# Bias and relu of a feed-forward moved to ScalarE, the 8-bit copy to VectorE, and a new table of times

## The chip, the cores and the metric

The kernel runs on one core of one Trainium2 chip. A core has five engines that run on their own: TensorE (PE in the profile, with its weight loads as PEld), VectorE (DVE), ScalarE (ACT), GpSimd (POOL) and SyncE (SP), which here issues nearly all DMAs. Each engine is given its instructions in the order in which the program records them; between engines, semaphores make a reader wait for its writer and a writer for the last reader of what it overwrites. The metric is the device time of the program in microseconds, the median of several runs.

## The reference

The input is 64 images of 96 channels, 56 x 56. Layer 0 is a convolution block: a 1x1 expansion to 192 channels with silu, a shift and shuffle of channel groups, a depthwise 3x3, silu, a squeeze-and-excite gate, a 1x1 projection and a residual. Layer 1 takes the 3136 pixels as tokens, normalizes them, mixes them in a two-dimensional frequency domain (here as matrix products with tables), and adds that to the tokens. The last part is a quantized feed-forward:

```python
def _qlinear(x, W, b):
    y = q_acc(jnp.einsum('bsk,nk->bsn', q_mul(x), q_mul(W)))   # 8 bit in, sum rounded to 16 bit
    return q_acc(y + q_mul(b))                                 # sum with the bias, rounded to 16 bit
h = jax.nn.relu(_qlinear(x, W1, b1))                           # 96 -> 384
y = _qlinear(h, W2, b2)                                        # 384 -> 96
```

`q_mul` rounds to a float with 5 exponent and 2 mantissa bits (fp8e5), `q_acc` to one with 5 and 10 (f16). So the hidden layer needs, in this order: the product rounded to f16, the bias added and rounded to f16, relu, and a rounding to fp8e5 for the second product.

## The kernel before

The work on an image is cut into some 60 kinds of steps, each a small function with an image number `b` and a part number `i`. Names end in `_mm` for matrix products on PE, and mostly in `_ev` for the evictions of their results from PSUM. The stages, in the order of an image's way through them:

- `x_in`, `ea_mm`, `ea_ev`, `eb_mm`, `eb_ev`, `eb_sh`, `eb_z`: load, expansion with silu (ACT); `eb_sh` shifts channel groups by DMAs on SP, `eb_z` clears border columns on POOL.
- `dw_mm`, `dw_ev`, `gt`, `gs`, `lt`, `ls`: the depthwise filter, in part as PE products, in part as nine taps each on DVE (`gt` L489 and L487, `lt` L502 and L500); the sums in `dw_ev`, `gs`, `ls` go to the gate.
- `se1_*`, `se2_*`: the gate. `se2_pw` (L552, DVE) folds it into the projection's weights, once per image.
- `pj_mm`, `pj_add` (L587, DVE), `pj_ev` (L593, ACT): projection and residual, into the token tile `t`.
- `c_mm`, `c_st`, `c_v`, `c_pow`, `sp_v` (L655, DVE), `sp_mm`, `sp_ev`, `sp_st`: statistics of the first normalization, in two halves; `c_pow` is a power on POOL.
- `w1_mm`, `w1_ev` (L686, DVE), `f1_mm`, `f1_ev`, `f1_st`: first mix, first transform, results to DRAM.
- `f2_ld` (SP), `f2_mm`, `f2_u` (L770, ACT), `f2_s` (L786 and L789, DVE), `f2_r` (L793, ACT), `f2_p` (L799, DVE): second transform with a complex product and relu, in six groups. A group has a tile `ue` with two halves, which `f2_u` writes one after the other and `f2_s` reads and rewrites.
- `w2_*`, `i1_*`, `i2_ld` (SP), `i2_mm`, `i2_ev` (L896, DVE): second mix and the way back, added to `t`.
- `n_*`, `x_*`: second normalization, tokens as fp8e5 (`n_pow` L912 on POOL, `n_x` L919 on ACT).
- the feed-forward, in 7 groups of 8 rows with 3 parts each, so 21 times per image: `h_mm` (L939, PE), `h_ev` (L944, ACT: PSUM to 16 bit), `h_b` (L949), `h_q` (L955); then per group `o_mm` (L961, PE), `o_ev` (L966, ACT), `o_b` (L971, ACT: second bias, in 16 bit), `o_f` (L977, DVE: residual), `o_st` (SP).

Before, `h_b` adds the bias and takes the maximum with 0 on DVE, in place on the 16-bit tile, and `h_q` copies that tile to fp8e5 on ACT.

The order of all steps is written in a table. `PLAN` has for every step and part a time, and `PERIOD` the distance of two images; all steps of all 64 images are recorded in the order of `b * PERIOD + when`:

```python
for _, b, k, i in sorted(
    (b * PERIOD + when, b, k, i)
    for b in range(NB)
    for k, step in enumerate(STEPS)
    for i, when in enumerate(PLAN[step.__name__])
):
    STEPS[k](b, i)
```

So the times are only sort keys: nothing waits for a clock. With times from -9 to 428 and a PERIOD of 105, parts of five images are interleaved on each engine, and one pass through the order, from one `se2_pw` to the next, holds each step of an image once. The PSUM tiles are few: two large buffers are used in turn by `w1`, `f1`, `f2`, `w2`, `i1` and `i2`, and four small ones in turn by all other products.

Of the kernel before, what the change touches and what calls it, by code (L numbers as in the profile page):

```python
# [10 lines left out]
AF = mybir.ActivationFunctionType  # L11
ALU = mybir.AluOpType
# [29 lines left out]

PERIOD = 105.0000000
PLAN = {
    "x_in": (-5.6038637, -8.8381554, 6.2538794, 1.1812168, 16.3290193, 18.2852724, 6.8664140),
    "ea_mm": (71.3166402, 9.9626057, 70.7451177, 21.6750117, 65.3314579, 73.1081582, 53.0001125),
    "ea_ev": (71.4998900, 11.8833092, 70.9831361, 25.0494290, 65.3324579, 75.4760214, 54.7839542),
    "eb_mm": (20.7568939, 18.2862724, 20.0880579, 17.7349364),  # L50
    "eb_ev": (23.7980033, 19.7804381, 20.6194508, 17.7359364),
    "eb_sh": (30.1373485, 40.4268576, 27.1837130, 37.9131670),
    "eb_z": (47.6742308,),
    "dw_mm": (77.9546249, 77.9556249, 80.7234624),
    "dw_ev": (84.6664508, 84.5735370, 85.4255761, 84.6664508),
    "gt": (
        72.3773055, 76.5125929, 80.2867409, 80.6441083, 81.5978867, 83.3027644, 84.6020247, 85.5619425, 86.6358385,
    ),
    "gs": (87.3111062,),
    "lt": (  # L60
        47.4152368, 51.7884497, 60.4614124, 63.7966655, 70.3566676, 70.7623183, 72.0563386, 78.2533320, 82.6592559,
    ),
    "ls": (84.0968675,),
    "se1_mm": (88.1632442,),
    "se1_ev": (88.3332823,),
    "se2_mm": (89.5466763,),
    "se2_ev": (90.4665288,),
    "se2_th": (90.7934716,),
    "se2_pw": (92.0502895,),
    "pj_mm": (94.5530355, 94.5540355, 102.0867331, 102.0877331),  # L70
    "pj_add": (95.2755331, 97.5636980, 96.0830143, 95.1836140, 106.8994545, 105.9451741, 104.6876054, 105.6968155),
    "pj_ev": (95.9050131, 100.2006242, 96.8964656, 97.4087014, 107.1621768, 108.5177420, 105.3642695, 105.8415338),
    "c_mm": (108.8639612, 112.5088807, 112.0440542, 109.4090967, 116.6350776, 116.2904132, 135.7736125),
    "c_st": (109.9566474, 113.8485179, 113.0437550, 111.6043666, 127.2877074, 117.1026522, 137.4879453),
    "c_v": (113.8495179, 141.3061112),
    "c_pow": (113.8505179, 141.3071112),
    "sp_v": (118.0429167, 144.9541062),
    "sp_mm": (119.0531042, 154.1921897),
    "sp_ev": (120.1871679, 157.1439845),
    "sp_st": (130.9824656, 157.1449845),  # L80
    "w1_mm": (140.5452441, 132.6482511, 135.8336192, 137.4906636, 166.3523765, 171.4972169, 172.4722919),
    "w1_ev": (143.0235958, 134.1359263, 138.9251145, 141.6196817, 167.5676600, 175.3749595, 176.4038215),
    "f1_mm": (145.6274382, 150.9380879, 155.6433445, 167.0161422, 169.8440182, 175.7343775, 181.4398534),
    "f1_ev": (147.8032262, 153.3968496, 159.4311586, 168.6496602, 170.8773139, 175.7353775, 183.1217269),
    "f1_st": (156.9268876, 156.9278876, 159.7610134, 170.1776408, 177.2523722, 181.0963765, 183.4782115),
    "f2_ld": (187.2815556, 187.2825556, 187.2835556, 188.6871659),
    "f2_mm": (191.1567314, 194.9032982, 192.7760178, 198.9093529, 201.4926219, 207.3412304),
    "f2_u": (
        191.1577314, 191.6562889, 197.1245553, 197.1783541, 193.2014504, 193.4636961, 199.3778915, 199.4257855,
        202.6220676, 205.9228992, 210.6728919, 211.5690444,  # L90
    ),
    "f2_s": (
        192.4250284, 193.9349638, 197.4091017, 197.4101017, 194.5789035, 195.6210358, 199.5749065, 199.8323547,
        205.9228992, 207.2409149, 211.9521364, 211.9531364,
    ),
    "f2_r": (193.9359638, 199.3441286, 197.3984294, 206.6372292, 207.5062232, 214.4127396),
    "f2_p": (196.9933570, 199.5074020, 198.4889191, 207.7927174, 209.1210238, 217.7061307),
    "w2_mm": (200.3894916, 200.0698788, 211.3168798, 219.8206887),
    "w2_ev": (201.9237699, 200.2428780, 213.5686424, 221.6127349),
    "i1_mm": (203.1484168, 217.0192486, 223.8701013),  # L100
    "i1_ev": (207.4757051, 209.2393192, 221.2926416, 218.5724351, 226.9503254, 225.7919736),
    "i1_st": (227.4371665, 231.7746699, 237.1127120),
    "i2_ld": (247.3246163, 258.4005613),
    "i2_mm": (247.3256163, 248.9786662, 258.4015613, 258.4015613),
    "i2_ev": (248.8862636, 249.1565727, 251.6982706, 252.2464870, 259.1359643, 258.4025613, 264.6426220, 261.8850697),
    "n_mm": (253.7316943, 255.9231087, 254.3994689, 265.3165318, 262.8490081, 267.4335438, 274.2854929),
    "n_sq": (253.7326943, 256.4684950, 254.9830489, 267.2212265, 263.8196833, 269.2996327, 274.6498815),
    "n_v": (253.7336943, 257.7773358, 255.3268787, 271.2717974, 268.7188670, 272.3139830, 278.4419729),
    "n_pow": (253.7346943, 262.7040095, 256.0602786, 275.1413670, 271.5489182, 273.1976811, 278.5569536),
    "n_x": (259.5582250, 262.7050095, 260.5027085, 276.7536912, 273.5135570, 275.1181728, 279.4588576),  # L110
    "x_mm": (259.5592250, 267.5155107, 260.5037085, 277.7892684, 276.4517499, 277.1023738, 280.0425162),
    "x_ev": (262.4788526, 271.3250083, 262.9497100, 279.9343023, 277.5776996, 279.5752541, 280.9231813),
    "h_mm": (
        282.1072054, 281.8171435, 284.3242143, 283.3068688, 297.0889770, 299.9198326, 301.6559190, 316.8088320,
        330.1509260, 345.7814283, 348.2910018, 350.2353211, 296.8878517, 323.5297033, 341.8803208, 341.1070144,
        349.1164583, 347.9208679, 316.7096209, 337.5767067, 324.7962443,
    ),
    "h_ev": (
        284.9055256, 281.8181435, 286.7711359, 286.2538800, 300.1659528, 301.6061574, 301.6569190, 319.9246149,
        331.0399476, 346.4058862, 354.2442780, 353.1416746, 297.2413855, 326.1086749, 343.4780845, 342.6875640,  # L120
        356.9377387, 352.1488917, 318.6795915, 341.2226048, 328.4873812,
    ),
    "h_b": (
        285.4467375, 285.0084677, 291.2143255, 290.3869640, 307.4021554, 308.1480888, 315.5861436, 337.9149029,
        341.4422638, 351.7638454, 354.2452780, 353.3258891, 302.2808169, 326.8831223, 346.3774903, 342.6885640,
        357.2985996, 352.4379170, 320.6635037, 341.2236048, 337.0905654,
    ),
    "h_q": (
        290.1888952, 290.1898952, 292.3650273, 291.6620769, 314.5146883, 319.2434525, 328.1869035, 340.6025047,
        344.9455204, 354.3021981, 356.7052110, 375.6421815, 326.8831223, 326.8841223, 346.3869475, 346.7213238,  # L130
        374.1067707, 366.6357739, 325.5334877, 345.8789179, 337.3330982,
    ),
    "o_mm": (297.2153719, 323.2068041, 391.0564841, 383.7794044, 346.7502251, 401.7878092, 346.4614096),
    "o_ev": (299.2426704, 325.5592410, 392.9287695, 385.0364968, 346.9425985, 404.8006504, 346.4624096),
    "o_b": (302.4327810, 325.5602410, 395.0955840, 397.1802374, 347.8135349, 407.2015543, 351.0696253),
    "o_f": (325.1830475, 327.1074074, 398.6818786, 400.3662261, 357.3959208, 411.4278754, 351.6615662),
    "o_st": (340.2945764, 339.2746723, 424.0034698, 405.1739043, 379.1046584, 427.6733014, 390.2778445),
}


# [1 line left out]
def conv_attn_ffn(  # L142
# [36 lines left out]
    nc = tc.nc  # L179
# [157 lines left out]
    qb1 = const.tile([128, 3], F32, name="qb1")  # L337
# [40 lines left out]
    held = {}  # L378
# [567 lines left out]

    def h_b(b, i):
        y16 = held["y", b, i]
        nc.vector.tensor_scalar(y16, y16, qb1[:, i % 3 : i % 3 + 1], 0.0, ALU.add, ALU.max)  # L949

    def h_q(b, i):
        j, m = divmod(i, 3)
        if m == 0:
            held["h8", b, j] = work.tile([128, 3, CH], F8, tag="h8", name="h8", bufs=3)
        nc.scalar.copy(held["h8", b, j][:, m, :], held.pop(("y", b, i)), saturate=False)  # L955

    def o_mm(b, j):
        h8 = held.pop(("h8", b, j))
# [21 lines left out]
    def o_st(b, j):  # L980
# [6 lines left out]
        w1_mm, w1_ev, f1_mm, f1_ev, f1_st, f2_ld, f2_mm, f2_u, f2_s, f2_r, f2_p, w2_mm, w2_ev, i1_mm, i1_ev, i1_st,  # L987
        i2_ld, i2_mm, i2_ev,
        n_mm, n_sq, n_v, n_pow, n_x, x_mm, x_ev, h_mm, h_ev, h_b, h_q, o_mm, o_ev, o_b, o_f, o_st,
    )  # L990

    with tc.manual_schedule():
# [3 lines that stand above are left out]
# [183 lines left out]
```

## Time and profile before

| | us |
|---|---|
| three runs | 6437.04, 6433.02, 6433.70 |
| median | 6433.7 |
| the profiled execution | 6434.72 |
| its span, first to last instruction | 6432.9 |
| PE busy | 5903.3 |
| DVE busy | 5452.4 |
| ACT busy | 5003.9 |
| POOL busy | 1159.1 |

The mean granted clock of TensorE was 0.984. Rows of the profile name a line of the kernel, an engine, an operation, the tile written and those read, the shape, a count, then busy time and the mean of one in ns, and the idle time of the engine in front of such instructions with what ended it. Rows of a timeline give the start in us from the span's beginning, the length in us, and then the instruction; "x2" merges two in a row.

### The profile page before, as it was taken

Reading aid. Unit: us, or ns where it says so; the run is one execution under the profiler, and the core shown is the slowest. Engines: PE = TensorE matmul, PEld = TensorE weight load, DVE = VectorE, ACT = ScalarE, POOL = GpSimd, SP = SyncE. Lnnn points to the kernel's source line nnn. Section 1 sums busy time; section 2 is a strip of 40 time slices with the busy share of each in tenths; the row PEclk is TensorE's granted clock in tenths of the full one; section 3 lists DMA queues with packets and bytes.
Section 4 is the critical chain, followed back from the end, with each engine's and each line's share of the span. In section 5 each row is a group of like instructions: output and inputs, shape, how many; then the busy total and the mean of one; then the engine's idle time right before and its main releaser. Section 6 shows DMA issues by size and latency. Waiting matters only on the chain.

```text
span 6432.9 us, 215622 instructions
## 1 busy us (share of the span) xinstructions
PE 5903.3 (92%) x92162; PEld 3939.1 (61%) x92162; DVE 5452.4 (85%) x10386; ACT 5003.9 (78%) x10830; POOL 1159.1 (18%) x652
## 2 busy tenths in 40 slices
PE   5999999999999999999999999999999999999996
PEld 3666666666666666666666666666666666666664
DVE  6788888888888888888988888888888888888885
ACT  2677778778777787777787787878877877878777
POOL 1112112112112111121121121211211211211211
PEclk8999999999999999999999999999999999999997
DMA  3344434444444444344444443443443444444433
GB/s 93 109 117 127 125 110 133 122 118 127 121 122 127 115 127 125 110 131 119 117 129 123 121 126 113 130 121 113 132 125 112 130 124 117 127 117 129 121 108 92
DMA packets 665511, 772.70 MB, mean 120 GB/s; under 512 B 273104, under 2 KB 591256, under 8 KB 664424
## 3 DMA queue, kind: packets, MB, share of 16 engines
q1 hardware_dynamic: 661832, 757.14, 41.8%
q8 instruction: 724, 11.86, 0.8%
q10 hardware_dynamic: 2720, 1.77, 0.1%
q14 instruction: 235, 1.93, 0.1%
HBM read 349.05 MB, written 354.16 MB: 109 GB/s over the span
## 4 chain that ended last, share of the span: by engine, by line
DVE 29%; PE 27%; ACT 13%; POOL 12%; DMA 11%; issue 5%; SPq 2%; POOLq 0%; DVEq 0%; ACTq 0%
POOL rs L912 8%; DVE d_vec L489 7%; DMA buf_g<-rows 6%; POOL rs L650 4%; PE psa L849 4%; DMA buf_g<-spec 4%; DVE t L896 3%; DVE d_last L502 3%; DVE ue L789 3%; DVE s L786 3%; ACT ue L770 3%; PE ps_pj L568 3%; PE psa L810 2%; PE ps_pj L579 2%; PE ps_eb L415 2%
## 5 line engine op out<-in xcount | busy, mean ns | idle before, releaser
L650 POOL TENSOR_TENSOR rs<-v,mhalf 128x16 f32<-128x16 f32 (+1 forms) x128 | 384.7, 3006 | 4385.6 <-DVE v L645 4385.6
L955 ACT CAST h<-y 128x448 fp8e5<-128x448 f16 x1344 | 749.0, 575 | 286.8 <-DVE y L949 286.8
L502 DVE SCALAR_TENSOR_TENSOR d_last<-e_b,taps,d_last 128x1568 f32<-128x1568 f32 x512 | 944.0, 1844 | 0.5
L912 POOL TENSOR_TENSOR rs<-v,mhalf 128x4 f32<-128x4 f32 x448 | 741.7, 1760 | 818.9 <-DVE v L617 784.0
L489 DVE SCALAR_TENSOR_TENSOR d_vec<-e_a,taps,d_vec 128x1120 f32<-128x1120 f32 x512 | 707.1, 1381 | 2.7
L949 DVE TENSOR_SCALAR y<-y,qb 128x448 f16<-128x448 f16 x1344 | 424.9, 329 | 324.8 <-ACT y L944 318.0
L944 ACT CAST y<-ps_h 128x448 f16<-128x448 f32 x1344 | 674.6, 539 | 26.9 <-PE ps_h L939 26.9
L681 PE MATMUL psa<-w1c,t 112*128 112x192 f32 x3584 | 669.0, 330 | 2.8 <-DMA t<-dev_t 2.8
L468 PE MATMUL ps_d<-e_a,diag 32*32 32x504 f32 x18432 | 628.6, 590 | 1.5 <-issue 1.4
L681 PEld LDWEIGHTS psa<-w1c,t 112*128 112x128 f32 x3584 | 592.5, 190 | 22.4 <-ACT fs L713 3.0
L468 PEld LDWEIGHTS ps_d<-e_a,diag 32*32 32x32 f32 x18432 | 410.5, 103 | 200.7 <-ACT y L944 37.3
L745 PE MATMUL psa<-l_tab,buf_g 128*64 128x112 f32 x7424 | 425.3, 267 | 113.9 <-DMA buf_g<-spec 87.9
L745 PEld LDWEIGHTS psa<-l_tab,buf_g 128*64 128x64 f32 x7424 | 369.5, 140 | 250.4 <-DMA buf_g<-spec 131.5
L919 ACT ACTIVATE xt<-ps_n,rs 128x96 fp8e5<-128x96 f32 x1792 | 454.4, 346 | 72.5 <-POOL rs L912 65.9
L686 DVE SCALAR_TENSOR_TENSOR buf_h<-psa,rs 128x768 f32<-128x768 f32 x448 | 425.5, 950 | 55.0 <-PE psa L681 54.6
L977 DVE TENSOR_TENSOR o<-t,o 112x448 f32<-112x448 f32 x448 | 418.8, 935 | 21.8 <-ACT o L971 19.5
L786 DVE SCALAR_TENSOR_TENSOR s<-psa,fa,ue 128x448 f32<-128x448 f32 (+1 forms) x512 | 325.2, 635 | 117.3 <-ACT ue L770 112.8
L593 ACT ACTIVATE t<-ps_pj,pjbn_b 112x504 f32<-112x504 f32 (+1 forms) x512 | 300.5, 619 | 150.2 <-DVE ps_pj L587 150.2
L400 PE MATMUL ps_ea<-x,ex_w 112*32 112x448 f32 x3584 | 416.1, 550 | 0.0
L770 ACT ACTIVATE ue<-psa,fa 128x448 f32<-128x448 f32 (+1 forms) x512 | 336.5, 686 | 100.0 <-DVE buf_h L799 57.7
L701 PE MATMUL psa<-buf_h,f_tab 56*64 56x384 f32 x3584 | 395.2, 509 | 17.6 <-DVE t L896 9.3
L810 PE MATMUL psa<-w2a,buf_h 128*64 128x96 f32 (+1 forms) x7424 | 358.9, 248 | 50.2 <-ACT buf_g L840 34.0
(171 smaller groups left out, 11865.9 us busy)
## 6 DMA issues: line engine op xcount, KB each, us to landing
spec<-fs SPq DMA_DIRECT2D x448, 384.0 KB
buf_g<-spec SPq DMA_DIRECT2D x192, 672.0 KB
out_dram<-o SPq DMA_DIRECT2D x448, 196.0 KB
buf_g<-rows SPq DMA_DIRECT2D x128, 672.0 KB
x<-in_x SPq DMA_DIRECT2D x320, 203.0 KB
rows<-buf_g SPq DMA_DIRECT2D x128, 420.0 KB
rows<-buf_g SPq DMA_DIRECT2D x64, 504.0 KB
x<-in_x SPq DMA_DIRECT2D x128, 228.4 KB
```

The lines of the kernel that those rows point to most:

```text
L468: nc.tensor.matmul(pss[r][j * 32 : j * 32 + 32], lhsT=diag[pr, tap, :], rhs=e_a[pr, r0 : r0 + SR, dx : dx + HW], start=tap == 0, stop=tap ...
L489: nc.vector.scalar_tensor_tensor(d_vec, win, w, d_vec, ALU.mult, ALU.add)
L502: nc.vector.scalar_tensor_tensor(d_last, win, w, d_last, ALU.mult, ALU.add)
L650: nc.gpsimd.tensor_tensor(rs[:, js], v[:, js], mhalf[:, js], ALU.pow)
L681: nc.tensor.matmul(ps[:, k, 0:MID], lhsT=t[:, n0 : n0 + 2 * TP], rhs=w1c, start=True, stop=True)
L745: nc.tensor.matmul(ps[c0 : c0 + 64, k, 0:CP], lhsT=g_v[:, k1, c0 : c0 + 64], rhs=l_tab[:, k1, :], start=True, stop=True,)
L770: nc.scalar.activation(held["ue", b, i][:, q, 0:n, :], held["f2", b, i][:, 0:n, 0:HW], AF.Identity, bias=par[:, 2 + q : 3 + q], scale=par[ ...
L786: nc.vector.scalar_tensor_tensor(held["s", b, i][:, q, 0:n, :], im, par[:, m : m + 1], a, ALU.mult, ALU.add)
L810: nc.tensor.matmul(ps[c0:c1, u, k, 0:C], lhsT=pq_a[:, AT[k1], c0:c1], rhs=w2a, start=k == 0, stop=False, skip_group_check=True,)
L912: nc.gpsimd.tensor_tensor(rs, held.pop(("nv", b, g)), mhalf[:, 0:4], ALU.pow)
L944: nc.scalar.copy(y16, held.pop(("h", b, i)))
L955: nc.scalar.copy(held["h8", b, j][:, m, :], held.pop(("y", b, i)), saturate=False)
```

## The change

`h_b` becomes an ACT activation, relu with the bias as its argument, in place on the same 16-bit tile; `h_q` becomes a DVE copy from that tile to fp8e5. The names and lines stay. `PERIOD` and the times of all steps in `PLAN` are new; `pj_mm` keeps its four parts. The diff, with the table cut to the rows of which the text speaks:

```diff
-PERIOD = 105.0000000
+PERIOD = 102.2951152
 PLAN = {
...
-    "eb_sh": (30.1373485, 40.4268576, 27.1837130, 37.9131670),
-    "eb_z": (47.6742308,),
+    "eb_sh": (-17.6154500, -15.9127200, -24.0315800, -15.6905400),
+    "eb_z": (-7.7850900,),
...
-    "c_mm": (108.8639612, 112.5088807, 112.0440542, 109.4090967, 116.6350776, 116.2904132, 135.7736125),
+    "c_mm": (59.4587800, 60.0115300, 62.0418600, 60.7653300, 67.0208600, 62.6719000, 65.2556000),
...
-    "sp_v": (118.0429167, 144.9541062),
+    "sp_v": (68.5601600, 79.5835800),
...
-    "w1_ev": (143.0235958, 134.1359263, 138.9251145, 141.6196817, 167.5676600, 175.3749595, 176.4038215),
+    "w1_ev": (80.9797500, 83.0191200, 93.3324800, 87.2346800, 105.1838200, 111.0812800, 97.2977000),
...
     "f2_u": (
-        191.1577314, 191.6562889, 197.1245553, 197.1783541, 193.2014504, 193.4636961, 199.3778915, 199.4257855,
-        202.6220676, 205.9228992, 210.6728919, 211.5690444,
+        138.0540500, 138.0550500, 147.6787200, 148.3315400, 140.6491200, 142.2848100, 150.8378500, 151.8766800,
+        154.9088200, 155.0511900, 159.5374300, 160.6034600,
     ),
     "f2_s": (
-        192.4250284, 193.9349638, 197.4091017, 197.4101017, 194.5789035, 195.6210358, 199.5749065, 199.8323547,
-        205.9228992, 207.2409149, 211.9521364, 211.9531364,
+        140.3886900, 140.3896900, 149.4147700, 150.2843900, 143.5489500, 143.7516700, 151.6466600, 152.4316700,
+        155.3184000, 156.4887900, 161.3532300, 161.3542300,
     ),
...
-    "i2_ld": (247.3246163, 258.4005613),
+    "i2_ld": (180.1612300, 188.5926300),
...
-    "i2_ev": (248.8862636, 249.1565727, 251.6982706, 252.2464870, 259.1359643, 258.4025613, 264.6426220, 261.8850697),
+    "i2_ev": (185.9837900, 185.9837900, 186.7002400, 187.1144600, 191.7293400, 191.1283000, 195.0233515, 194.8050300),
...
     "h_ev": (
-        284.9055256, 281.8181435, 286.7711359, 286.2538800, 300.1659528, 301.6061574, ...
+        229.1094900, 228.7612101, 239.7382600, 228.8131600, 244.2390900, 246.5362800, ...
     "h_b": (
-        285.4467375, 285.0084677, 291.2143255, 290.3869640, 307.4021554, 308.1480888, ...
+        230.6722300, 236.0710000, 242.1428400, 233.1143800, 249.6670900, 258.1373100, ...
...
-    "o_b": (302.4327810, 325.5602410, 395.0955840, 397.1802374, 347.8135349, 407.2015543, 351.0696253),
+    "o_b": (283.1918300, 273.6047100, 352.4743700, 303.5309500, 292.8660900, 336.4152500, 287.7771600),
-    "o_f": (325.1830475, 327.1074074, 398.6818786, 400.3662261, 357.3959208, 411.4278754, 351.6615662),
+    "o_f": (286.8041800, 279.1551200, 358.2985100, 313.3837400, 297.8003600, 339.2981000, 289.8053900),
...
@@ def h_b, def h_q
     def h_b(b, i):
         y16 = held["y", b, i]
-        nc.vector.tensor_scalar(y16, y16, qb1[:, i % 3 : i % 3 + 1], 0.0, ALU.add, ALU.max)
+        nc.scalar.activation(y16, y16, AF.Relu, bias=qb1[:, i % 3 : i % 3 + 1])
 
     def h_q(b, i):
         j, m = divmod(i, 3)
         if m == 0:
             held["h8", b, j] = work.tile([128, 3, CH], F8, tag="h8", name="h8", bufs=3)
-        nc.scalar.copy(held["h8", b, j][:, m, :], held.pop(("y", b, i)), saturate=False)
+        nc.vector.tensor_copy(held["h8", b, j][:, m, :], held.pop(("y", b, i)), saturate=False)
```

On DVE the order of one pass is, around the places of which the text speaks: before, `sp_v[0]` h_b 20, c_st 4, h_b 7, 19, 8, 15, w1_ev 1, h_b 14, c_st 6, w1_ev 2, c_v 1, w1_ev 3, o_f 6, h_b 9, 17, w1_ev 0, h_b 11, `i2_ev[0]`; after, `sp_v[0]` h_q 6, 7, 19, o_f 1, h_q 20, 13, c_v 1, sp_v 1, h_q 14, w1_ev 0, o_f 0, w1_ev 1, h_q 15, 17, 16, `i2_ev[0]`.

On SP, before: sp_st 0, i1_st 2, eb_sh 2, eb_sh 0, i2_ld 0, eb_sh 3, eb_sh 1, i2_ld 1; after: i1_st 2, sp_st 0, o_st 2, o_st 1, i2_ld 0, eb_sh 2, eb_sh 0, i2_ld 1, eb_sh 1, eb_sh 3. On POOL, before: n_pow 0, n_pow 2, eb_z, n_pow 1; after: n_pow 0, n_pow 2, n_pow 1, eb_z.

## The prediction

> **What bounds the kernel now.** I read the engine sums first, then the chain that ended last.
>
> ```profile
> span 6432.9 us, 215622 instructions
> PE 5903.3 (92%) x92162; PEld 3939.1 (61%) x92162; DVE 5452.4 (85%) x10386; ACT 5003.9 (78%) x10830; POOL 1159.1 (18%) x652
> DVE 29%; PE 27%; ACT 13%; POOL 12%; DMA 11%; issue 5%; SPq 2%; POOLq 0%; DVEq 0%; ACTq 0%
> ```
>
> No engine is full, and the chain passes through all of them: a fixed order on each engine is waiting round a loop. The loop is one image. The instruction at L552 (`se2_pw`) runs once per image, 64 times, from 82.0 to 6241.7 us, so an image takes 6159.7 / 63 = 97.8 us, and 82.0 before and 191.2 after lie outside the loop. I cut one undisturbed image, from L552 to L552, at two joints where the chain changes engines: `sp_v` (L655, first half) and the first `i2_ev` (L896).
>
> ```profile
> 4087.03:4119.66 32.63, 30.47 (x405) 19.54 (x401) 27.42 (x70) 25.07 (x45) 3.77 (x1) 1.00 0.35 105
> 4119.66:4134.50 14.84, 14.17 (x149) 10.09 (x150) 8.83 (x28) 12.40 (x27) 2.27 (x1) 1.00 0.71 167
> 4134.50:4184.37 49.87, 47.37 (x890) 31.21 (x887) 48.48 (x64) 40.79 (x97) 11.84 (x8) 0.97 0.43 123
> ```
>
> Columns after the length: PE, weight loads, DVE, ACT, POOL busy. Stretch A (32.6) is a ping-pong of PE, DVE and ACT. In B (14.8) DVE is 60% busy and ACT 84%. In C (49.9) DVE is busy 48.5: **C lasts as long as its DVE work**, and has 1.4 of idle. So DVE work moved from B to C is not free, though DVE as a whole has 12.6 us of idle per image (97.34 - 84.73).
>
> The waits that matter, from the timelines of ACT and DVE in this image (start, length, what, idle before):
>
> ```profile
> 4087.14 1.34 ACT L770 ACTIVATE ue<-psa,fb 128x448 f32<-128x448 f32 x2 [0.79 <-DVE buf_h L799]
> 4092.40 1.34 ACT L770 ACTIVATE ue<-psa,fa 128x448 f32<-128x448 f32 x2 [0.90 <-DVE buf_h L799]
> ```
> ```profile
> 4088.52 0.69 DVE L786 SCALAR_TENSOR_TENSOR s<-psa,fb,ue 128x448 f32<-128x448 f32 x1 [0.39 <-ACT ue L770]
> 4093.77 0.68 DVE L786 SCALAR_TENSOR_TENSOR s<-psa,fa,ue 128x448 f32<-128x448 f32 x1 [0.40 <-ACT ue L770]
> 4125.84 0.83 DVE L949 TENSOR_SCALAR y<-y,qb 128x448 f16<-128x448 f16 x3 [4.85 <-ACT y L944]
> ```
>
> The first `f2_s` of a group starts not behind the first `f2_u`, but behind **both**: the two end at 4087.14 + 1.34 = 4088.48, and DVE starts at 4088.52; again 4093.74 and 4093.77. Both halves share one tile `ue`, and an access waits for all earlier writes of the tile. The third line is the big hole of B.
>
> **The moved operations, priced.**
>
> ```profile
> L955 ACT CAST h<-y 128x448 fp8e5<-128x448 f16 x1344 | 749.0, 575 | 286.8 <-DVE y L949 286.8
> L949 DVE TENSOR_SCALAR y<-y,qb 128x448 f16<-128x448 f16 x1344 | 424.9, 329 | 324.8 <-ACT y L944 318.0
> L971 ACT ACTIVATE o<-o,qb 112x448 f16<-112x448 f16 x448 | 291.7, 665 | 4.2
> ```
> ```profile
> L333 DVE CAST q<-fw x1: 351/351/351, 33.6 to 33.6; 96x384 fp8e5<-96x384 f32 x1
> L336 DVE CAST q<-fw x1: 325/325/325, 36.6 to 36.6; 128x336 fp8e5<-128x336 f32 x1
> ```
>
> *`h_b` on ACT.* Nearest row: L971, same function with a bias, 16 bit to 16 bit, 448 elements: 665 ns against the 575 of the cast that leaves: +90 ns x 21 = +1.9 us of ACT per image. ACT has 19 idle; only what falls in B counts (below).
>
> *`h_q` on DVE.* Two casts to 8 bit in the set-up give (351 - 325) / 48 = 0.54 ns per element, so 351 + 64 x 0.54 = 386 ns at 448: +57 ns against 329, x 21 = +1.2 us of DVE. [...] Back to back, starts lie closer than durations (three L949 take 0.83, so 0.25 each); 386 becomes 0.31.
>
> **The new order, stretch by stretch.** Times in the table are sort keys; an image's key has its number times PERIOD added, so keys are compared after whole PERIODs are taken off.
>
> *A: +0.5.* `o_b[2]` (352.47 - 204.59 = 147.88) now stands on ACT between `f2_u[2]` (147.68) and `f2_u[3]` (148.33). DVE's next instruction is `f2_s[2]`, which waits for both: one L971 back to back, +0.6. Then `f2_s[6]` (151.65) is recorded ahead of `f2_u[7]` (151.88), where before it came behind. Now `f2_u[7]` writes a tile that `f2_s[6]` writes, so it waits for DVE, and `f2_s[7]` for it: 1.4 + 0.72 + 1.4 and two handovers, 3.6, for the old 0.40 of wait + 2.7 = 3.1: +0.5. The end of `f2_s[7]` is 1.1 late; behind it wait `w2_mm[0]` (same PSUM buffer), all eight `pj_add`, and `c_mm`, which already waits 0.93 for the last `pj_ev`. Of the 1.1 I give back 0.6: `c_mm` 0, 1, 3 now stand together ahead of `i1_mm[1]`, so one transpose group instead of two follows it before the statistics, and `h_b[18]` no longer stands between the `c_st`. Ends: -0.6 (the waits fall into A's 5.2 of DVE idle) and +1.1.
>
> *B: -0.8.* `i2_ld[0]` moves on SP ahead of the `eb_sh`, which wait for `eb_ev`; on SP it now follows `sp_st[0]`, `o_st[2]`, `o_st[1]` and can go 4 us earlier. But `i2_mm[0]` still stands on PE behind three `ea_mm`, four `eb_mm`, two `w1_mm` and the `h_mm`, and these wait for PSUM buffers that ACT empties. ACT from `sp_v` on: 0.75 to `sp_ev`'s end, six `h_ev` x 0.42 = 2.5, five `h_b` x 0.58 = 2.9, three `ea_ev` 1.35, four `eb_ev` 1.9, `o_b` 0.57, `sp_ev` 0.25, `o_ev` 0.53 = 10.75, plus 1.0 waiting for the `eb_mm` = 11.75; then `h_mm[10]`, `o_mm[4]`, `i2_mm[0]` 0.2 + 0.6 + 1.3 and latencies 0.2: 14.05 for 14.84. Ends: -1.6, +0.3. So the 4.85 hole is moved (in front of `w1_ev[0]`), not filled.
>
> *C: +3.1.* More DVE work stands between `i2_ev[0]` and L552: `w1_ev` 2 and 3 (keys 93.3, 87.2 against 83.7 for `i2_ev[0]`; all of 0 to 3 were ahead before): 2 x 0.87 = 1.74. Four `o_f` instead of three: 0.85. Eight `h_q` x 0.31 instead of six `h_b` x 0.25: 0.98. `sp_v[1]` leaves: -0.09. Sum 3.5. At the end `h_b[2]` and `h_ev[4]` stand ahead of `f2_u[5]` (0.58 + 0.42), for which `f2_s[4]` waits; `h_q[2]` (0.31) fills part: +0.7. Of C's old idle of 1.4 I let the added work fill 1.1: 3.5 + 0.7 - 1.1 = 3.1. Ends 2.8 and 4.2.
>
> *Counted at nothing:* `eb_z` falls behind `n_pow[1]` on POOL, and `lt[1]` waits for it; `i2_ev`, `o_f`, `w1_ev[2]` stand between on DVE, 2.8 us, more than the 1.8 of a power; without that cover up to 1.5. `f1_ev[6]` falls behind six ACT evictions, so `f1_st[6]` and the four `f2_ld` behind it on SP go about 1 us later; PE waits longer for them (87.9 us in all now), but `f2_s` then waits for `gs`, which DVE's last taps set.
>
> Sum per image: 0.5 - 0.8 + 3.1 = **+2.8 us**, x 63 = +176. The profiled execution took 6434.7 (span 6432.9 and 1.8 around it), 1.0 above the median of 6433.7; start and end I leave. 6433.7 + 176 = **6610 us**, +2.7%.
>
> **Rivals.**
> 1. *Faster: the earlier row load decides B.* If B ends with the load and not with ACT, it shrinks by the load's gain: 4.6 us (issue from 4127.1 to about 4122.5). Then 0.5 - 4.6 + 3.1 = -1.0 per image: 6370. It decides from 3.6 us of shrinkage on. For it: DMA share is 0.71 in B, its highest. Against: PE and ACT are busy 14.2 and 12.4 of 14.8 there, and B's ACT work doesn't shrink.
> 2. *A's waits are absorbed.* A changes by -0.6 instead of +0.5: +1.7, 6540. For it: 5.2 us of DVE idle in A; against: 2.2 of that is another wait for `f2_u`, further down the same chain.
> 3. *The 8-bit copy runs at one element per cycle.* Nearest row: L799, 128x448 f32, 617 ns: 0.23 more x 8 in C = 1.9, and some 0.8 in A and B: +5.5, 6780. Against: the set-up casts have half that slope.
> 4. *Nothing moves:* more and less cancel within 0.2%.
>
> **How the numbers follow.** Chances: main case 0.71, rival 1 0.13, rival 2 0.09, rival 3 0.05, rival 4 0.02. Slower by over 0.2% (what this kernel's measurements can tell from no change): 0.85; faster 0.13; same 0.02. The ends of A, B and C add up to +0.6 and +5.6 per image; half-way to both, +1.7 to +4.2, is the main case's own range: 6540 to 6700. Range for 8 in 10: down to the sum of all lower ends (6433.7 + 63 x 0.6 = 6470), up to C's end with the rule's price for the copy on top (+4.7: 6730); rivals 1, 3 and 4 are left out: **6470 to 6730**.
>
> **What would show it.** L552 to L552 near 100.6 us. DVE busy up 1.2 per image, ACT 1.9; L955 on DVE near 386 ns, L949 on ACT near 665. An `f2_u[7]` that waits for DVE's L789, and a longer wait of L786 for L770. DVE nearly without idle from the first L896 to L552, over 52 us. The prediction is wrong if A ends earlier than 32 us, if the first L896 comes under 12 us after L655, or if DVE has several us of idle in C.

## The result and the profile after

The changed kernel takes 6499.6 us (median of four runs, 6495.3 to 6507.4) against 6433.6 for the kernel before in the same session: a ratio of 1.0103, 95% interval 1.0085 to 1.0120. So it is slower by 1.0%. The prediction said slower, +176 us; measured were +66. The sign was right; the size forecast was 2.7 times the size measured.

The page of the kernel after, its span, the engine sums and the chain that ended last:

```profile
span 6493.2 us, 215180 instructions
PE 5962.9 (92%) x92162; PEld 3936.4 (61%) x92162; DVE 5520.0 (85%) x10386; ACT 5121.1 (79%) x10830; POOL 1040.0 (16%) x652
PE 48%; DVE 22%; ACT 19%; POOL 5%; DMA 4%; issue 2%; SPq 1%; POOLq 0%; ACTq 0%; DVEq 0%
```

DVE has 68 us more work and ACT 117, or 1.06 and 1.83 per image, close to the forecast of 1.2 and 1.9. But in the chain POOL and DMA fell from 12% and 11% to 5% and 4%, and PE went from 27% to 48%. POOL's own work fell by 119 us, though on POOL only the place of `eb_z` changed. Of this, 49 us are the power of the first normalization (L650), which is taken up below, and 70 the powers of the second (L912, from 741.7 to 671.8), whose part in the result was not tried. Nothing in the prediction provided for that.

The two operations that changed engines, from the groups of the kernel after (busy us, mean ns, idle before):

```profile
L949 ACT ACTIVATE y<-y,qb 128x448 f16<-128x448 f16 x1344 | 876.1, 672 | 8.4
L955 DVE CAST h<-y 128x448 fp8e5<-128x448 f16 x1344 | 486.1, 386 | 209.4 <-ACT y L949 209.3
```

They take 672 and 386 ns; 665 and 386 were forecast. So the prices of the operations are not what failed.

The line of `se2_pw` in the kernel after (count, duration ns least/median/most, first and last start):

```profile
L552 DVE SCALAR_TENSOR_TENSOR pw<-gate,pj_w x64: 848/850/857, 83.8 to 6294.6; 128x672 f32<-128x672 f32 x64
```

(6294.6 - 83.8) / 63 = 98.58 us per image, against 97.77: +0.81 x 63 = +51. The first one is 1.8 later, and from the last one to the end it is 198.6 instead of 191.2, +7.4. Together that is +60, the difference of the two spans.

An image of the kernel after that lies near the mean, cut at the same joints (length, PE, weight loads, DVE, ACT, POOL busy; the last three numbers are the granted clock, the DMA share and GB/s):

```profile
2039.85:2071.64 31.79, 29.78 (x402) 20.12 (x398) 26.76 (x75) 25.07 (x44) 2.97 (x1) 1.00 0.30 91
2071.64:2084.19 12.55, 12.55 (x144) 7.23 (x144) 7.26 (x20) 12.18 (x27) 2.27 (x1) 1.00 0.69 172
2084.19:2138.77 54.58, 49.38 (x910) 33.12 (x907) 51.68 (x69) 42.67 (x100) 10.64 (x8) 1.00 0.43 125
```

B and C of an image of the kernel before that lies near its mean:

```profile
2741.02:2756.23 15.21, 14.17 (x149) 10.09 (x150) 8.83 (x28) 12.39 (x27) 2.27 (x1) 1.00 0.72 163
2756.23:2806.11 49.88, 46.23 (x902) 31.04 (x899) 48.39 (x64) 40.62 (x97) 11.84 (x8) 1.00 0.41 121
```

The means over the 40 images from the 13th to the 52nd, cut in the same way:

| stretch | before | after | change | predicted |
|---|---|---|---|---|
| A | 32.76 | 31.93 | -0.83 | +0.5 (-0.6 to +1.1) |
| B | 15.23 | 12.57 | -2.66 | -0.8 (-1.6 to +0.3) |
| C | 50.17 | 54.49 | +4.32 | +3.1 (2.8 to 4.2) |
| sum | 98.16 | 98.99 | +0.83 | +2.8 |

All three left their ranges: C, where the loss was expected, loses more than forecast; A and B, which were to come out near even, give back 3.5. So A and B need an explanation first. In B the second line of the kernel after shows what the prediction did not: PE is busy 12.55 of 12.55 us.

### The profile page after: what moved, and what is told of

It is laid out like the page before. It is cut to its first block, busy times and chain, and to the rows that moved or that the text cites. A ratio compares the mean times of both kernels' runs of the same rounds, so it can differ in the third digit from the quotient of the medians.

```text
span 6493.2 us, 215180 instructions
## 1 busy us (share of the span) xinstructions
PE 5962.9 (92%) x92162; PEld 3936.4 (61%) x92162; DVE 5520.0 (85%) x10386; ACT 5121.1 (79%) x10830; POOL 1040.0 (16%) x652
## 4 chain that ended last, share of the span: by engine, by line
PE 48%; DVE 22%; ACT 19%; POOL 5%; DMA 4%; issue 2%; SPq 1%; POOLq 0%; ACTq 0%; DVEq 0%
PE ps_d L468 8%; PE psa L681 5%; PE psa L849 5%; POOL rs L912 5%; ACT ue L770 4%; DVE ue L789 4%; DVE s L786 4%; PE psa L810 4%; DVE buf_h L799 3%; ACT y L944 3%; PE ps_c L623 3%; DVE buf_h L686 3%; PE ps_eb L415 3%; PE ps_n L601 3%; PE ps_ea L400 2%
## 5 line engine op out<-in xcount | busy, mean ns | idle before, releaser
L650 POOL TENSOR_TENSOR rs<-v,mhalf 128x16 f32<-128x16 f32 (+1 forms) x128 | 335.2, 2619 | 3870.7 <-DVE v L645 3870.7
L912 POOL TENSOR_TENSOR rs<-v,mhalf 128x4 f32<-128x4 f32 x448 | 671.8, 1500 | 1496.5 <-DVE v L617 1113.7
L949 ACT ACTIVATE y<-y,qb 128x448 f16<-128x448 f16 x1344 | 876.1, 672 | 8.4
L955 DVE CAST h<-y 128x448 fp8e5<-128x448 f16 x1344 | 486.1, 386 | 209.4 <-ACT y L949 209.3
L468 PEld LDWEIGHTS ps_d<-e_a,diag 32*32 32x32 f32 x18432 | 369.6, 103 | 299.1 <-ACT e_a L405 100.6
L745 PE MATMUL psa<-l_tab,buf_g 128*64 128x112 f32 x7424 | 425.4, 268 | 71.8 <-DMA buf_g<-spec 39.9
L793 ACT ACTIVATE s<-s 128x896 f32<-128x896 f32 (+2 forms) x384 | 343.0, 893 | 161.9 <-DVE s L786 161.8
L939 PE MATMUL ps_h<-xq,q 96*128 96x448 fp8e5 x1344 | 390.5, 357 | 81.7 <-ACT d L477 70.6
L713 ACT COPY fs<-psa 128x768 f32<-128x768 f32 x448 | 361.0, 806 | 87.5 <-PE psa L701 79.8
L810 PEld LDWEIGHTS psa<-w2a,buf_h 128*64 128x64 f32 (+1 forms) x7424 | 320.4, 131 | 178.6 <-issue 144.2
```

The lines of the kernel that those rows point to most:

```text
L468: nc.tensor.matmul(pss[r][j * 32 : j * 32 + 32], lhsT=diag[pr, tap, :], rhs=e_a[pr, r0 : r0 + SR, dx : dx + HW], start=tap == 0, stop=tap ...
L745: nc.tensor.matmul(ps[c0 : c0 + 64, k, 0:CP], lhsT=g_v[:, k1, c0 : c0 + 64], rhs=l_tab[:, k1, :], start=True, stop=True,)
L810: nc.tensor.matmul(ps[c0:c1, u, k, 0:C], lhsT=pq_a[:, AT[k1], c0:c1], rhs=w2a, start=k == 0, stop=False, skip_group_check=True,)
L912: nc.gpsimd.tensor_tensor(rs, held.pop(("nv", b, g)), mhalf[:, 0:4], ALU.pow)
L949: nc.scalar.activation(y16, y16, AF.Relu, bias=qb1[:, i % 3 : i % 3 + 1])
```

## The experiments

Times are medians; a ratio is to the kernel before on the same chip, with its 95% interval. "Mean" is always over the same 40 images.

### B: the load of the rows, and PE

**e8, the load alone.**

```diff
 # before
-    "i2_ld": (247.3246163, 258.4005613),
+    "i2_ld": (237.1500000, 258.4005613),
```

> The kernel before with one key changed: i2_ld[0] ahead of the first two eb_sh on SP, as the change has it. In the kernel before, B is 14.41 us where the first L884 does not wait, and up to 16.6 where it waits for the rows. Theory (the prediction's rival 1 in part: the load ends B in most images): the wait goes, B from 15.2 on average to 14.4, -0.8 x 63 = -50, 6384. Rival (B is set by PE and ACT, and the load arrives anyway): 6434 within 10. If the eb_sh, now later, hold up the taps: above 6450.

Measured: 6397.6 us, 0.9946 (0.9934 to 0.9958). The mean of B falls from 15.23 to 14.43, and 37 of the 40 images now lie within 0.01 of 14.41; before they were strewn from 14.41 to 17.68. One line of the waits says why (us in total, times, longest), first in the kernel before, then in the kernel after:

```profile
PE psa L884 <- DMA buf_g<-rows: 43.7, 51, 2.8
```
```profile
PE psa L884 <- DMA buf_g<-rows: 4.0, 6, 1.4
```

In 51 cases the first product of the way back waited for the rows. In the kernel after that wait has nearly gone. So the load did end B, by 0.8 us on average. The image that the prediction cut had B at 14.84, and in it this product waited only 0.35 us. The trace names L949 for that wait, but the instruction on SP that waits for the rows goes on 0.1 us earlier, and e8 takes the wait away. The image was "undisturbed", but not the mean. The gain in time, 35 us, is below the 50 expected; in the profiled execution C is 0.1 us longer, and the image as a whole shorter by 0.66 instead of 0.8.

**e12, the load put back in the kernel after.**

```diff
 # after
-    "i2_ld": (180.1612300, 188.5926300),
+    "i2_ld": (180.6000000, 188.5926300),   # behind eb_sh[2]
```

> The kernel after with one key changed: i2_ld[0] on SP behind eb_sh[2], so that it waits for the eviction eb_ev[2] and is issued some 3 us later. Theory (in the kernel after the rows arrive only just ahead of the first L884, which in e8 took up to 7 us from the issue; so the earlier load is what lets B be as short as its PE work): B from 12.6 to 14.5 to 16, +2 to +3.4 per image, 6625 to 6715. Rival (B is set by PE alone and the load arrives anyway): 6500 within 15.

Measured: 6755.9 us, 1.0503 (1.0487 to 1.0519), +256 over the kernel after and above the theory's range. Waits of PE, and the stretch B of an image near the mean:

```profile
PE psa L884 <- DMA buf_g<-rows: 194.8, 63, 5.2
```
```profile
3178.62:3194.87 16.25, 13.37 (x142) 8.01 (x142) 7.31 (x20) 13.87 (x30) 2.27 (x1) 0.94 0.53 132
```

B is 16.26 on average instead of 12.57, +3.7, and nearly every image waits about 3 us for the rows (194.8 us in 63 cases); A and C add another 0.4. The other 0.6 us of B is slower work: behind the wait the granted clock falls, to 0.95 on average over B where it was 1.00, and a product of L884 takes 264 ns on average instead of 212. So the early load is worth 0.8 us per image in the old order and 3.7 in the new one: there the rest of B has become so short that the rows arrive just in time. In the median the load is issued 7.1 us after L655 before, 4.3 after, 8.0 here, and 5.5 in e8. It moved by 2.8 us and not by the 4.6 that rival 1 took. Of the missing 1.8, 0.8 is a wait in its new place, where SP holds it back until the store of the rows has landed:

```profile
SPq L874 <- DMA rows<-buf_g: 54.2, 64, 2.2
```

**e5, two products put back into B.**

```diff
 # after
-    "w1_mm": (79.0596500, 82.1139300, 91.8888400, 86.1581900, ...
-    "w1_ev": (80.9797500, 83.0191200, 93.3324800, 87.2346800, ...
+    "w1_mm": (79.0596500, 82.1139300, 82.1160000, 82.1140000, ...
+    "w1_ev": (80.9797500, 82.1150000, 83.0200000, 82.1170000, ...
```

> The kernel after with w1_mm and w1_ev of groups 2 and 3 put back ahead of the first i2_ev. Theory (B is now as long as its PE work, 12.55 busy of 12.55 us, and C as long as its DVE work): B grows by the two w1_mm, 2 x 1.47 = 2.9 us, and C shrinks by the two w1_ev, 1.74: +1.2 x 63 = +76, about 6575. Rival (B ends with ACT's evictions, as the prediction had it, and has room on PE): B as it is, C -1.74: 6390.

Measured: 6584.8 us, 1.0240 (1.0223 to 1.0256), where the theory had 6575. B and C of an image near the mean:

```profile
3102.70:3118.01 15.31, 15.31 (x160) 9.80 (x160) 9.24 (x22) 12.62 (x28) 2.27 (x1) 1.00 0.77 191
3118.01:3170.98 52.97, 47.21 (x894) 30.32 (x891) 50.05 (x66) 42.17 (x99) 10.89 (x8) 1.00 0.40 115
```

B grows by 2.75 (mean) and PE fills it again without a gap; the two `w1_mm` are 2.9 us of PE work. C shrinks by 1.5 (mean) for two `w1_ev` of 0.87. **In the kernel after, B is as long as its PE work.** The prediction took the two `w1_ev` into C and priced them there; that their products leave B on PE, 2.9 us, does not stand in its sum for B at all. They are not the whole change on PE: two more `ea_mm`, 1.5 us, come into B, and smaller pieces leave, so that PE's work there falls by 1.55 in all, from 14.10 (mean of e8) to 12.55. That accounts for B's -2.66: 0.80 was the wait for the rows, 1.55 is PE's work, and 0.31 is a wait of PE for L655 at the start of B, which the new order fills.

### A: an order that costs, and a power that ends late

**e4, the order of `f2_u` and `o_b` undone.**

```diff
 # after
-    "o_b": (283.1918300, 273.6047100, 352.4743700, ...      f2_u[7]: 151.8766800
+    "o_b": (283.1918300, 273.6047100, 352.9300000, ...      f2_u[7]: 151.6460000
```

> The kernel after with two keys changed: o_b of column group 2 behind f2_u[3] instead of between f2_u[2] and f2_u[3], and f2_u[7] ahead of f2_s[6] as it was before. Theory (PE has no idle between the first w2_mm and the first c_mm after the change, so the 1.0 us by which f2_s[7] ends earlier comes through to sp_v[0]): A from 31.8 to 30.8, 6500 - 63 = 6437. Rival (the waits are absorbed in A, as the predicted +0.5 did not show): f2_s[7] earlier by 1.0 and sp_v[0] by less than 0.2, 6490 to 6500.

Measured: 6434.6 us, 0.9998 (0.9990 to 1.0007): **two keys take away the whole loss of the change.** These are the instructions in the kernel after, on ACT and on DVE, in the image from 2237.00 (start, length, idle before):

```profile
2239.10 0.69 DVE L786 SCALAR_TENSOR_TENSOR s<-psa,fb,ue 128x448 f32<-128x448 f32 x1 [1.26 <-ACT ue L770]
2246.06 0.68 DVE L786 SCALAR_TENSOR_TENSOR s<-psa,fa,ue 128x448 f32<-128x448 f32 x1 [0.79 <-ACT ue L770]
```
```profile
2245.31 0.72 ACT L770 ACTIVATE ue<-psa,fa 128x448 f32<-128x448 f32 x1 [1.60 <-DVE ue L789]
```

`f2_s[2]` waits 1.26 where it waited 0.39, and `f2_u[7]` waits 1.60 for DVE: the two effects that the prediction named. Followed through A (medians, us after L552):

| | before | after | e4 |
|---|---|---|---|
| end of `f2_s[7]` | 9.46 | 10.47 | 9.52 |
| first `c_mm` | 22.97 | 23.31 | 22.37 |
| `c_v[0]` (L641) | 27.93 | 27.89 | 26.95 |
| `sp_v[0]` (L655) | 32.63 | 31.79 | 30.85 |

The delay is 1.0 at the end of `f2_s[7]` (forecast 1.1), and e4 shows that nearly all of it reaches `sp_v[0]`: 0.94. It is not absorbed; it is paid for by others. Up to `c_v[0]` 1.0 is given back (from +1.01 to -0.04), where 0.6 was forecast for the order of `c_mm` and `h_b[18]`. Of it, 0.67 comes ahead of the first `c_mm`, where PE waited 0.93 us for the last `pj_ev` before and has other work now, and only 0.38 behind it, where that order can act. And from `c_v[0]` to `sp_v[0]`, where only the power on POOL stands, it takes 3.90 instead of 4.70.

**e1, one addition away from the power.** Beside that power, in the kernel before:

```profile
4115.69 0.94 DVE L977 TENSOR_TENSOR o<-t,o 112x448 f32<-112x448 f32 x1
4115.86 3.77 POOL L650 TENSOR_TENSOR rs<-v,mhalf 128x16 f32<-128x16 f32 x1 [57.32 <-DVE v L645]
4116.55 0.32 DVE L949 TENSOR_SCALAR y<-y,qb 128x448 f16<-128x448 f16 x1
```

In the kernel after, the same power takes 2.97 us, and an 8-bit copy stands where the L977 stood:

```profile
2265.61 0.39 DVE L955 CAST h<-y 128x448 fp8e5<-128x448 f16 x1
2265.78 2.97 POOL L650 TENSOR_TENSOR rs<-v,mhalf 128x16 f32<-128x16 f32 x1 [55.28 <-DVE v L645]
```

In the kernel before, a second L977 ran at the end of the power, and e1 moves that one.

```diff
 # before
-    "o_f": (325.1830475, 327.1074074, ...
+    "o_f": (325.1830475, 338.0000000, ...
```

> The kernel before, with one addition (o_f of column group 1) moved from just ahead of sp_v[0] into the 4.85 us hole behind it. Theory P (the power on POOL in A waits for a DVE instruction with two operands in SBUF): L650 of 16 columns falls from 3.77 to 2.97 us, A from 32.6 to 31.8, and as the hole of B takes the addition, the time falls by 0.8 x 63 = 50 us to about 6384. Rival (the power is shorter after the change for another reason, such as the 16-bit L949 that left DVE): L650 stays at 3.77, sp_v[0] where it is, 6434.

Measured: 6482.3 us, 1.0068 (1.0056 to 1.0081), and L650 stays at 3.77. The theory fails on both. The addition at the power's end does nothing. And the loop became longer, by 0.5 in B (mean 15.74): the moved addition is followed on SP by its store, and behind that store stands `sp_st[0]`, now issued 3.1 us after L655 instead of 0.9. PE then waits 0.23 us per image for what `sp_st[0]` stores; where the rest of the 0.5 comes from was not tried.

What is left is the DVE work that is under way when the power begins. Across the runs, the 16-column power ends 2.76 us after the end of the run of additions (L977), 16-bit passes (L949) and 8-bit copies (L955) on DVE that is under way when it begins. "Run" means that each begins before the one ahead has ended. In the median that run ends 1.01 us after POOL's start before (0.69 + 0.32; the power takes 3.77), 0.22 after (2.97), 0.16 in e3 (2.92), and 1.38 in e2, where two 8-bit copies follow the addition (4.13). Normalization statistics (L631), which read PSUM, run beside it and don't delay it: in the kernel after, 0.75 us of them follow the 8-bit copy without a break, and the power takes 2.97 us all the same. The run must be unbroken, as e6 (below) shows, which makes every copy twice:

```profile
1537.54 0.39 DVE L955 CAST h<-y 128x448 fp8e5<-128x448 f16 x1
1537.71 2.97 POOL L650 TENSOR_TENSOR rs<-v,mhalf 128x16 f32<-128x16 f32 x1 [57.39 <-DVE v L645]
1537.96 0.39 DVE L956 CAST h<-y 128x448 fp8e5<-128x448 f16 x1
```

The second copy starts 0.03 us after the first has ended, and the power still ends 2.76 us after the first: behind a break of 0.03 us the next copy no longer moves the power's end.

**e9, both additions away.**

```diff
 # e8
-    "o_f": (325.1830475, 327.1074074, ...    "o_st": (340.2945764, 339.2746723, ...
+    "o_f": (338.0000000, 338.1000000, ...    "o_st": (345.2000000, 345.3000000, ...
```

> The kernel before with i2_ld[0] ahead (as in e8, 6398) and both additions o_f of groups 0 and 1 moved from around POOL's power in A into the hole of B, their two stores on SP behind the first two eb_sh, so that sp_st[0] is not held up as in e1. Theory P2 (the power cannot start to read while DVE works without a pause on instructions with two operands in SBUF or on 16-bit copies; it takes 2.76 us from the end of that run): with only one L949 of 0.33 behind c_v[0], L650 of 16 columns falls from 3.77 to 2.91, A from 32.65 to 31.8, B stays at 14.4: 6398 - 0.85 x 63 = 6344. Rival (the length of the power has another cause): L650 stays at 3.77, 6398.

Measured: 6468.8 us, 1.0066 (1.0054 to 1.0079). The power takes 2.90 and A 31.76 (median), as expected; but B is 16.44 on average, 2.0 more than in e8. The waits ahead of L977 in this kernel:

```profile
  DMA out_dram<-o: 111.7, 61
```

61 times, 1.8 us each, `o_f[6]` waits for a store: it writes one of two `o32` buffers, and that buffer's old store had been moved back too. As in e1, the addition was moved without counting what its store does.

**e11, the stores in their right place.**

```diff
 # e9
-    "o_st": (345.2000000, 345.3000000, ...
+    "o_st": (342.1200000, 342.1300000, ...   # just ahead of i2_ld[0]
```

> e9 with the two stores o_st of groups 0 and 1 on SP just ahead of i2_ld[0], which there waits for the store of the rows anyway. In e9 the power shrank to 2.90 us and A to 31.76, but B grew by 1.9, because o_f[6] waited 1.8 us for a buffer that the late stores still read. Theory: A stays at 31.8, B goes back to 14.4: 6398 - 0.87 x 63 = 6343. Rival (the hole of B cannot take two additions, or the stores run into the load of the rows): B 15 or more, 6385 or above.

Measured: 6353.7 us, **0.9881 (0.9864 to 0.9897): faster than both kernels**, with the old engines and five changed keys. The power with what stands beside it, from a timeline, and the three stretches of an image:

```profile
1347.65 2.90 POOL L650 TENSOR_TENSOR rs<-v,mhalf 128x16 f32<-128x16 f32 x1 [57.32 <-DVE v L645]
1347.95 0.34 DVE L949 TENSOR_SCALAR y<-y,qb 128x448 f16<-128x448 f16 x1 [0.38 <-ACT y L944]
```
```profile
1318.83:1350.59 31.76, 29.61 (x403) 19.36 (x400) 25.81 (x69) 24.53 (x44) 2.90 (x1) 1.00 0.35 106
1350.59:1365.40 14.81, 14.81 (x143) 10.31 (x143) 10.65 (x30) 12.96 (x29) 2.27 (x1) 1.00 0.71 174
1365.40:1415.54 50.14, 46.45 (x909) 31.37 (x905) 48.40 (x64) 40.65 (x97) 11.91 (x8) 1.00 0.40 120
```

A is 0.9 shorter than before, and the power fits what was found above: a 16-bit pass that begins 0.3 us after it no longer matters. B is 14.81 and not 14.41: as A ends earlier, 0.9 us of PE work (L849) that fell into A falls into B, and only 0.3 of it fits into the gap that PE had at the start of B. So of the 0.9 gained in A, 0.4 is lost again in B.

### C: DVE's work, and the end of the stretch

**e6, more of the work that is in dispute.**

```diff
 # after
+        nc.vector.tensor_copy(held["h8", b, j][:, m, :], held["y", b, i], saturate=False)
         nc.vector.tensor_copy(held["h8", b, j][:, m, :], held.pop(("y", b, i)), saturate=False)
```

> The kernel after with every 8-bit copy on DVE made twice (21 more instructions of 386 ns per image, 0.31 apart; 8 of them in C). Theory (C lasts as long as its DVE work): C +8 x 0.31 = +2.5, A and B take most of the other 13 in their idle time (0 to +1.5): +2.5 to +4.0 per image, 6657 to 6750. Rival (C is set by a chain through PE and ACT, and DVE's 51.7 of 53.9 only lies beside it): C under +1, 6500 to 6560.

Measured: 6809.4 us, 1.0587 (1.0573 to 1.0601), above the theory's range. C is 56.57 on average, +2.1, and not the +1 at most of the rival: it does follow DVE's work, but not in full, since here a second copy starts 0.42 us after its first and not 0.31, which is 3.4 us for eight. So DVE's work is most of what sets C, not all. A takes +0.8 and B +2.0, where 0 to 1.5 was expected of both together. From a timeline of DVE at the end of B, the first and the last copies and the first `i2_ev`:

```profile
1549.79 0.40 DVE L955 CAST h<-y 128x448 fp8e5<-128x448 f16 x1 [0.76 <-ACT y L949]
...
1554.97 0.39 DVE L956 CAST h<-y 128x448 fp8e5<-128x448 f16 x1
1555.28 1.15 DVE L896 SCALAR_TENSOR_TENSOR t<-psa,bn2c_b,t 112x392 f32<-112x392 f32 x2
```

DVE has 5.3 us of idle in B, but all of it lies ahead of this: behind the wait for the copy's `h_b` its queue is full, and four of the copies, 1.7 us more, stand ahead of the first L896. Idle time hides work only where it comes after the work is ready.

**e7 and e10, the two instructions ahead of `f2_u[5]`.**

```diff
 # e4
-    h_ev[4] 244.2390900   h_b[2] 242.1428400   h_q[2] 245.6766400
+    h_ev[4] 244.5950000   h_b[2] 244.5900000   h_q[2] 246.5500000
 # e10 in addition
-    o_mm[0] 246.6161000   o_ev[0] 248.4187700
+    o_mm[0] 254.9500000   o_ev[0] 255.9000000
```

> The kernel after with the order in A undone as in the run before (o_b of group 2 behind f2_u[3], f2_u[7] ahead of f2_s[6]; that alone gave 6435), and in addition h_b[2], h_ev[4] behind f2_u[5] on ACT and h_q[2] behind se2_ev on DVE. Theory (the prediction's +0.7 at the end of C): C from 53.9 to 53.2, 6435 - 44 = 6390. Rival (f2_s[4] waits for something else there, or the wait moves to the gate): 6435 within 12.

> e7 with o_mm[0] moved on PE behind pj_mm[1] and o_ev[0] on ACT behind pj_ev[1]. In e7 the 64 o_mm[0] waited 1.7 us each for the h_q[2] that had been moved back, and the gate's last step waited behind o_ev[0]. Theory (the prediction's +0.7 at the end of C exists, and e7 only put a new wait in its place): A back to 30.85, C to 53.2 to 53.4, 6435 - 0.6 x 63 = 6397. Rival (the end of C is set by the gate, and h_b[2] and h_ev[4] lie beside it): 6435 within 12.

Measured: e7 6567.0 us, 1.0211 (1.0196 to 1.0225); e10 6765.3 us, 1.0524 (1.0509 to 1.0539). Neither brought the gain that the theory had, and the waits of PE show what came in its place, first e7, then e10:

```profile
PE ps_o L961 <- DVE h L955: 110.2, 70, 4.0
```
```profile
PE ps_o L961 <- ACT t L593: 278.7, 62, 4.8
```

In e7 `o_mm[0]` waits on PE for the copy that was moved back, and A grows by 2.0. In e10 it stands where the next of the four small PSUM buffers is still held by a `pj_ev`, and waits 4.5 us. C itself is 54.43 in e7 and 54.12 in e10, against 54.39 in e4: of the 0.7 at most 0.3 came out. What the step is worth by itself stays open; both edits put a larger wait in its place. As in e12, the longer waits go with a lower clock: over A it is 0.96 on average in e7 and 0.93 in e10, where e4 has 1.00.

### Engines and table apart

**e2** has the old table with the new engines, **e3** the new table with the old ones.

```diff
 # e2: before, with the h_b and h_q of after (shown); e3: after, with those of before (the reverse)
-        nc.vector.tensor_scalar(y16, y16, qb1[...], 0.0, ALU.add, ALU.max)
-        nc.scalar.copy(held["h8", b, j][:, m, :], ...)
+        nc.scalar.activation(y16, y16, AF.Relu, bias=qb1[...])
+        nc.vector.tensor_copy(held["h8", b, j][:, m, :], ...)
```

> The old table of times with only the two operations exchanged between the engines. Theory (unit prices add up: DVE +1.1 and ACT +1.9 us per image, of which about 0.4 in C and 0.45 in B lie on the path): +0.9 x 63 = +55, 6490. Rival 1 (the table is the whole loss): 6434 within 15. Rival 2 (the exchange alone shortens the loop, because the copy behind bias and relu no longer crosses between engines twice and the 16-bit pass leaves DVE): below 6420.

> The new table of times with the old engines (relu in 16 bit on DVE, 8-bit copy on ACT). Theory (the table loses, the exchange costs some 0.9 us per image on top): 6500 - 55 = 6445. Rival 1 (the table is the whole loss): 6500 within 15. Rival 2 (the table was made for the new engines, and with the old ones the ping-pong between them stands in the way): above 6530.

Measured: e2 6781.6 us, 1.0538 (1.0522 to 1.0555); e3 6870.4 us, 1.0669 (1.0653 to 1.0685). Each half alone costs more than five times what both together do, and my theory, that unit prices add up, misses by 292 us for e2 and by 425 for e3. L955 and L949 take the same in e2 as after (386 and 672 ns); the time lies in waits. First e2, then e3:

```profile
DVE h L955 <- ACT y L949: 410.4, 266, 7.0
```
```profile
ACT h L955 <- DVE y L949: 655.6, 259, 7.7
DVE y L949 <- ACT y L944: 562.0, 207, 6.0
```

A table places `h_b` and `h_q` for the queue in which each stands. With the engines exchanged, the same key puts an instruction behind other neighbours, in both queues, and DVE and ACT wait for each other. So "what the operations cost" and "what the table costs" are no two parts of one sum here, and neither run says which part of the +66 belongs to which.

## Why the prediction was right in sign and wrong in size

*Unit prices.* Right: 672 ns (665) and 386 ns (386). The row of the set-up casts held. The upper end of the range, 6730, has 0.5 us per image on top of C's end (4.7 for 4.2), the "rule's price" of a dearer copy; no run shows that term: the copy took 386 ns in the kernel after and in e2, as the rows had it.

*A, +0.5.* The delay was right, 1.0 for 1.1, and it does come through (e4). What failed is "Of the 1.1 I give back 0.6": it was 1.0 up to `c_v[0]`, two thirds of it in a wait of PE that the prediction named and did not count as room, and then another 0.8 of which the sum knew nothing. The addition `o_f` beside `c_pow` left that place with the new table. I priced it as DVE work in C (0.85) and counted its leaving A as nothing, because A's chain goes through POOL there. It was on that chain all the same, through the late end of the power: with both additions away, the power takes 2.90 us instead of 3.77 and A of the old table gets 0.9 shorter (e9, e11).

*B, -0.8.* This is the largest error, 1.9 us per image and 117 us in all. The step that failed is the path of the sum: it ran along ACT's evictions to 14.05, with 1.0 for waits on `eb_mm` and the last `o_ev` and `h_b` on the path. B ended with the rows in most images before, 0.8 on average (e8), and with PE after (e5). ACT's work in B indeed did not shrink, 12.4 to 12.2 us; it did not set B's end. The missing term is PE's work in B: -1.55, of which the two `w1_mm` that leave are -2.9. The argument against rival 1, "PE and ACT are busy 14.2 and 12.4 of 14.8 there", took a full PE as a fixed floor, while the change itself lowered that floor to 12.55.

*Rival 1.* Its mechanism was half of the truth: without the early load B would be 3.7 us longer (e12). Its price of 4.6 was a distance between issue times in which the wait for the rows' own store (0.8) was left out, and it lacked PE's floor of 12.55.

*C, +3.1.* The added DVE work was right: 51.68 busy against 48.39 in the mean-like images, +3.3 for 3.5. The step that failed is "I let the added work fill 1.1" of the old idle: the idle grew instead. C has 2.8 us of DVE idle on average after and 1.8 before. Of the 1.0 more, 0.5 is a `w1_ev` that now waits for its product, and 0.3 the first `f2_s` of the stretch, which waits for `f2_u`. The wait of `f2_s[4]`, priced at +0.7, grew by 0.4 in the median (0.17 to 0.54) and by less than 0.1 in the mean (0.67 to 0.73).

*Counted at nothing.* That was right for `eb_z`: DVE's waits in front of `lt[1]` (L500) add up to 13 us before and 28 after, 0.2 more per image. PE's waits for the `f2_ld` fell from 87.9 us to 39.9, where longer ones were expected.

*Start and end, left out.* +1.8 and +7.4, together 9 of the 60 us by which the two profiled spans differ.

*The sum.* -1.3 in A, -1.9 in B and +1.2 in C turn +2.8 into +0.8 per image. Of the three signs of being wrong that the prediction lists, A under 32 us came true (31.93), and the first L896 less than 12 us after L655 nearly did (12.57). DVE's idle in C, 2.8 us, lies between the "nearly without" that it expected and the "several us" of the third sign.

## What to carry to other kernels

When a step is moved from one stretch to another, take it out of every engine's sum in the stretch that it leaves, the product as well as its eviction, and look again for what ends that stretch. Read a wait from all executions of the loop and not from one clean one: the wait that ended B cost 0.35 us in the image shown and 0.8 in the mean. And a result that moves by 1% can be the difference of two effects of 4%: two keys here were worth the whole loss, and five others took 77 us off the kernel before.

## What the runs showed of the hardware

The power on POOL took the longer, the longer DVE had work under way when it began, though the only wait in front of it in the profile is the one for L645. The power on 128x16 took 2.90 us with no such work beside its start (e9, e11), and otherwise ended 2.76 us after the unbroken run of additions, 16-bit passes or 8-bit copies that DVE had under way: it took 2.97 us (after), 3.77 (before) and 4.13 (e2). The other way round, no delay shows: in e11 a 16-bit pass starts 0.30 us after the power and takes its usual 0.34, in e6 an 8-bit copy starts 0.25 us after it and takes its usual 0.39, and in the kernel before an addition starts 1.42 us after the 12-column power and takes its usual 0.92, while the power stays at 2.27. What makes the power end late was not shown; the runs only changed which DVE work stands beside it.

In e12 a wait of PE cost more than its length. PE waits some 3 us there for the rows, and the granted clock falls: in one image it is 0.50 from 0.4 us behind the wait on, for 3.4 us. On average it is 0.95 over B instead of 1.00, and the products of L884 take 264 ns instead of 212, 0.6 us on top of the 3.1. The kernel after, which differs from e12 in one key, does not show it there.
